# Lane inverse of a gated delta rule: block products associated as (X22 M) X11 instead of X22 (M X11)

## The chip, the cores and the metric

The kernel runs on one core of a Trainium2 chip. The metric is the time of one execution on the device in microseconds (us). The profile names the engines PE (matmul; PEld is its weight load, which overlaps it), DVE (the vector engine), ACT (the scalar engine), POOL (GpSimd) and SP (which issues DMAs). Everything here is in 32-bit floats.

## The reference, cut to what matters

The reference is one transformer block with adaptive layer norm: 8 sequences of 512 rows and 256 columns go through a gated-delta-rule attention and then a mixture of experts with two of six chosen. Only the attention touches the change. For each of its 32 value heads the sequence is cut into chunks, and each chunk needs the inverse of a unit lower triangular matrix:

```
A = -where(strict_tril, einsum('bhnce,bhnde->bhncd', k_beta, kc) * decay, 0)
T = solve_triangular(eye - A, eye, lower=True)
value_      = T @ v_beta
k_cumdecay  = T @ (k_beta * exp(g)[..., None])
```

A scan over the chunks then carries a state of 128 x 128 for each head.

## The kernel before

The kernel uses chunks of 128 rows. A main loop runs over 128 iterations `n`, one for each of 8 sequences and 16 pairs of heads, in a software pipeline. In one turn of the loop it works on the keys of iteration n+9 (`keys`), on one quarter of a lane inverse (`diagonal_blocks`), on joining the inverse of iteration n+1 to full size (`join`), on the values of n+1 (`values`), on the recurrence of n (`recur`), and on the output of n-1 (`finish`). Each of these is a list of steps. `weave` (L52) merges the lists by their relative position, so that the steps of all of them alternate in the queues of the engines; the program's scheduler then settles the order of the single instructions. [...]

**The lane inverse.** One iteration has 2 heads and 4 chunks, so 8 matrices of 128 x 128, each with four 32 x 32 blocks on its diagonal. Four iterations make a group: 4 x 8 x 4 = 128 diagonal blocks. `leave` in `keys` (L648) writes them to DRAM, and `begin` (L707) reads them back so that each of the 128 lanes (partitions) holds one whole 32 x 32 block in `tl`, 1024 floats. DVE then inverts all 128 blocks at once, by elementwise products and sums along the free dimension. There are 32 such groups. `tl` holds a 32 x 32 block of A, called M here, transposed: element [c, r] of `tl` is element [r, c] of M. Two tiles hold the inverse: `xl` holds X by rows, and `yl` holds its transpose, so a row of `yl` is a column of X.

The inverse is built in four quarters, one for each turn of the loop:

- quarter 0: `begin`, then `row(1)` to `row(7)` (L714), which solve the four 8 x 8 blocks on the diagonal into `yl`, and `turn8` (L724), which copies them transposed into `xl`
- quarter 1: `join8_w` and `join8_x`, twice each, which join 8 x 8 blocks to 16 x 16
- quarter 2: `join16_w`, three times, the first product of the join from 16 to 32
- quarter 3: `join16_x`, three times, the second product, and `leave` (L773), which writes `xl` and `yl` to DRAM for `join`

A join fills the lower left block of an inverse whose diagonal blocks X11 and X22 are known: X21 = X22 M X11. Each of the two matrix products is done by a DVE multiplication of broadcast operands into `prl` (`e["pr"]`, up to 1024 products on each lane), and a DVE reduction over the innermost axis. The intermediate is kept in `wt`. Before the change, `join8_w` and `join16_w` form W = M X11, and `join8_x` and `join16_x` form X22 W. The helper `minus_m` (L698) returns a block of M from `tl` with its axes exchanged, so that the innermost axis, the one summed over, steps by one row of `tl`, 32 floats:

```
            def minus_m(r0, c0, nr, ncol):

                return part(e["t"], c0, r0, ncol, nr).rearrange("p c r -> p r c")
```

The lines that later sections name: L721 and L722 (product and reduction of `row`), L727 (`turn8`), L735 and L740 (product and reduction of `join8_w`), L751, L752 and L753 (product, reduction and transposed copy of `join8_x`), L760 and L765 (`join16_w`), L770 and L771 (`join16_x`), L775 (transposed copy in `leave`). Around them on DVE stand the convolutions (L513), the recurrence (`r` L927, `wd` L950, `st` L970 and L973, `o` L988 and L990), the output (`gt` L1046, the sum L1058), and one small instruction for each iteration at L1030.

Of the kernel before, what the change touches and what calls it, by code (L numbers as in the profile page):

```python
# [11 lines left out]
ALU = mybir.AluOpType  # L12
AX = mybir.AxisListType
# [49 lines left out]
def adaln_block(  # L63
# [369 lines left out]
    with ExitStack() as st:  # L433
# [11 lines left out]
        xl = w1b.tile([P, 32, 32], F32, name="xl")  # L445
        yl = w1b.tile([P, 32, 32], F32, name="yl")
# [234 lines left out]
        def diagonal_blocks(g):  # L681


            e = {}
            mul, red = nc.vector.tensor_tensor, nc.vector.tensor_reduce
            flat = lambda t: t.rearrange("p a b -> p (a b)")

            def part(t, r0, c0, nr, ncol):
                return t[:, r0 : r0 + nr, c0 : c0 + ncol]

            def diag8(t, r, c, nr, ncol):

                a = flat(t)
                return bass.AP(
                    a.tensor, a.offset + 32 * r + c, [list(a.ap[0]), [264, 4], [32, nr], [1, ncol]]
                )

            def minus_m(r0, c0, nr, ncol):  # L698

                return part(e["t"], c0, r0, ncol, nr).rearrange("p c r -> p r c")  # L700

            def bc(ap, axis, n):
                shape = list(ap.shape)
                shape.insert(axis, n)
                return ap.unsqueeze(axis).to_broadcast(shape)

            def begin():  # L707
                t = w1b.tile([P, 32, 32], F32, name=f"tl_{g}", tag="tl")
                nc.sync.dma_start(flat(t), groups[g]["t"])
                e["t"] = t  # L710
                e["wt"] = w1b.tile([P, 256], F32, name=f"wt_{g}", tag="wt")
                e["pr"] = w1b.tile([P, 1024], F32, name=f"prl_{g}", tag="prl")

            def row(i):  # L714
                y = diag8(yl, 0, i, i, 1)
                m = diag8(e["t"], 0, i, i, 1)
                if i == 1:
                    nc.vector.tensor_copy(y, m)
                    return
                pr = e["pr"][:, : 4 * i * i].rearrange("p (q c b) -> p q c b", q=4, c=i)  # L720
                mul(pr, diag8(yl, 0, 0, i, i), m.rearrange("p q b o -> p q o b").to_broadcast([P, 4, i, i]), ALU.mult)  # L721
                red(y.rearrange("p q c o -> p q (c o)"), pr, AX.X, ALU.add)  # L722

            def turn8():  # L724
                a = flat(xl)
                src = flat(yl)
                nc.vector.tensor_copy(  # L727
                    bass.AP(a.tensor, a.offset, [list(a.ap[0]), [264, 4], [32, 8], [1, 8]]),
                    bass.AP(src.tensor, src.offset, [list(src.ap[0]), [264, 4], [1, 8], [32, 8]]),
                )  # L730

            def join8_w(q):
                o = 16 * q
                pr = e["pr"][:, 512 * q : 512 * q + 512].rearrange("p (c a b) -> p c a b", c=8, a=8)
                mul(  # L735
                    pr, bc(minus_m(o + 8, o, 8, 8), 1, 8), bc(part(yl, o, o, 8, 8), 2, 8),
                    ALU.mult,
                )
                if q == 1:
                    red(  # L740
                        e["wt"][:, :128], e["pr"][:, :1024].rearrange("p (x b) -> p x b", b=8),
                        AX.X, ALU.add,
                    )

            def join8_x(q):
                o = 16 * q
                wt = e["wt"][:, 64 * q : 64 * q + 64].rearrange("p (c b) -> p c b", c=8)
                pr = e["pr"][:, 512 * q : 512 * q + 512].rearrange(
                    "p (a c b) -> p a c b", a=8, c=8
                )  # L750
                mul(pr, bc(part(xl, o + 8, o + 8, 8, 8), 2, 8), bc(wt, 1, 8), ALU.mult)  # L751
                red(part(xl, o + 8, o, 8, 8), pr, AX.X, ALU.add)  # L752
                nc.vector.tensor_copy(  # L753
                    part(yl, o, o + 8, 8, 8), part(xl, o + 8, o, 8, 8).rearrange("p a c -> p c a")
                )

            def join16_w(c, n, b):

                pr = e["pr"].rearrange("p (c a b) -> p c a b", c=n, a=16)
                mul(  # L760
                    pr, bc(minus_m(16, b, 16, 16 - b), 1, n), bc(part(yl, c, b, n, 16 - b), 2, 16),
                    ALU.mult,
                )
                wt = e["wt"].rearrange("p (c a) -> p c a", c=16)
                red(wt[:, c : c + n, :], pr, AX.X, ALU.add)  # L765

            def join16_x(a, n, w):
                pr = e["pr"].rearrange("p (a c b) -> p a c b", a=n, c=16)
                wt = e["wt"].rearrange("p (c b) -> p c b", c=16)
                mul(pr, bc(part(xl, 16 + a, 16, n, w), 2, 16), bc(wt[:, :, :w], 1, n), ALU.mult)  # L770
                red(part(xl, 16 + a, 0, n, 16), pr, AX.X, ALU.add)  # L771

            def leave():  # L773
                nc.sync.dma_start(groups[g]["x"], flat(xl))
                nc.vector.tensor_copy(  # L775
                    part(yl, 0, 16, 16, 16), part(xl, 16, 0, 16, 16).rearrange("p a c -> p c a")
                )
                nc.sync.dma_start(groups[g]["y"], flat(yl))

            return [  # L780
                [begin, *[lambda i=i: row(i) for i in range(1, 8)], turn8],
                [lambda: join8_w(0), lambda: join8_w(1), lambda: join8_x(0), lambda: join8_x(1)],
                [lambda: join16_w(0, 4, 0), lambda: join16_w(4, 4, 0), lambda: join16_w(8, 8, 8)],
                [
                    lambda: join16_x(0, 8, 8), lambda: join16_x(8, 4, 16),
                    lambda: join16_x(12, 4, 16), leave,
                ],
            ]

# [285 lines left out]
        for n in range(-LA, last + 2):  # L1075
# [18 lines left out]
            g, q = divmod(n + LA, 4)  # L1094
            if 0 <= g - 1 <= last // 4:
                if q == 0:
                    quarters = diagonal_blocks(g - 1)
                streams.append(quarters[q])
# [58 lines left out]
```

## Time and profile before

| | us |
|---|---|
| median of 3 runs | 4919.81 |
| lowest and highest of these | 4910.78, 4920.14 |
| the profiled execution's own time | 4912.86 |
| its span, from the first to the last instruction | 4911.1 |
| DVE busy in the products and reductions of the joins, L735 to L771 | 729.2 |

The last row sums the groups of those lines that have TENSOR_TENSOR or TENSOR_REDUCE as their operation. The granted clock of PE was 0.965 of full speed on average. The page of a profile gives each engine's busy time and how it is spread over the span; groups of instructions by line, with the mean duration of one; and the waits, that is, which instruction of which engine was late for which. Line numbers are those of the kernel before.

### The profile page before, as it was taken

How to read it: one execution, taken by the hardware profiler on the slowest of the kernel's cores; microseconds unless marked ns; L12 is line 12 of the kernel's file. 1: busy time of each engine (PE TensorE's matmuls, PEld its weight loads, DVE VectorE, ACT ScalarE, POOL GpSimd, SP SyncE). 2: the span in 40 equal slices, each digit the busy share in tenths (PEclk: the TensorE clock that was granted, in tenths of full speed). 3: DMA queues.
4: the chain of work that ended last, by engine and by line, in shares of the span. 5: the costliest groups of instructions: out<-in, count | busy, mean ns of one | idle time of the engine just before them, and what ended most of it. 6: DMA issues, size and time to landing. Idle time of an engine off the chain costs nothing. (4 is left out here: it accounts for less than half of the span.)

```text
span 4911.1 us, 84235 instructions
## 1 busy us (share of the span) xinstructions
PE 4569.8 (93%) x27112; PEld 3262.1 (66%) x27112; DVE 3815.8 (78%) x8513; ACT 3120.0 (64%) x8899; POOL 1826.3 (37%) x1708
## 2 busy tenths in 40 slices
PE   5599999999999999999999999999999999999998
PEld 3366666666666666676666666666666666666775
DVE  4678878877878778888788887788877887878864
ACT  4566666666666666676666665666755666666553
POOL 3333434334333334334334343333333334333311
PEclk8689999999999999999999999999999999999998
DMA  5555555555555555555454555555555555556431
GB/s 154 120 142 146 145 160 150 155 145 155 151 144 155 150 151 143 141 157 159 150 158 143 146 163 147 144 157 146 160 138 145 149 151 154 140 148 158 133 107 46
DMA packets 1045671, 712.91 MB, mean 145 GB/s; under 512 B 661105, under 2 KB 909809, under 8 KB 1045233
## 3 DMA queue, kind: packets, MB, share of 16 engines
q1 hardware_dynamic: 1044416, 705.69, 52.7%
q8 instruction: 219, 3.59, 0.3%
q14 instruction: 220, 1.79, 0.1%
q10 hardware_dynamic: 816, 1.84, 0.1%
HBM read 459.27 MB, written 247.99 MB: 144 GB/s over the span
## 5 line engine op out<-in xcount | busy, mean ns | idle before, releaser
L513 DVE SCALAR_TENSOR_TENSOR cvv<-prv,cw,cvv 128x511 f32<-128x511 f32 (+2 forms) x768 | 560.5, 742 | 19.8 <-ACT cvv L511 18.3
L996 ACT ACTIVATE jo<-o 128x128 f32<-128x128 f32 x1024 | 304.5, 298 | 386.1 <-DVE o L990 350.9
L1031 POOL TENSOR_TENSOR msq<-msq,mhalf 128x8 f32<-128x8 f32 x128 | 223.3, 1744 | 876.6 <-DVE msq L1030 758.4
L1053 PE MATMUL op<-wo,gt 128*128 128x256 f32 x2048 | 504.9, 385 | 28.4 <-DVE gt L1046 21.8
L1021 PE MATMUL prz<-ha,wz 128*128 128x512 f32 x1024 | 496.7, 607 | 14.8 <-DMA wz<-in_dram 12.0
L637 POOL TENSOR_TENSOR mta<-mta,dca 128x512 f32<-128x512 f32 x256 | 326.3, 1275 | 466.6 <-DVE mta L626 429.4
L503 PE MATMUL prv<-ha,wv 128*128 128x512 f32 x1024 | 492.9, 603 | 4.9 <-DVE cvk L513 4.7
L604 ACT ACTIVATE dca<-gb,G 128x128 f32<-128x128 f32 x1024 | 334.8, 392 | 239.5 <-DMA sfar<-dca 179.8
L1053 PEld LDWEIGHTS op<-wo,gt 128*128 128x128 f32 x2048 | 370.6, 191 | 101.5 <-DVE gt L1046 37.4
L956 ACT ACTIVATE w<-u,br 128x128 f32<-128x128 f32 x1024 | 320.5, 361 | 164.3 <-DVE wd L950 130.0
L567 POOL TENSOR_TENSOR nrmk<-nrmk,half 128x4 f32<-128x4 f32 x128 | 140.9, 1101 | 741.3 <-ACT jk L563 727.5
L639 POOL TENSOR_TENSOR dca<-qkm,dca 128x256 f32<-128x256 f32 x512 | 387.6, 778 | 18.7 <-DVE qkm L631 0.6
L982 PEld LDWEIGHTS in<-w,s 128*128 128x128 f32 x2048 | 312.4, 197 | 92.7 <-issue 55.5
L982 PE MATMUL in<-w,s 128*128 128x128 f32 x2048 | 337.4, 287 | 4.3 <-ACT w L956 4.3
L617 PE MATMUL kk<-kqa 128*128 128x256 f32 x1024 | 314.2, 419 | 26.0 <-ACT kqa L527 14.6
L964 PE MATMUL dst<-wd,kr 128*128 128x256 f32 x768 | 265.7, 428 | 77.0 <-DVE wd L950 52.2
L513 DVE SCALAR_TENSOR_TENSOR cvk<-prk,cw,cvk 128x511 f32<-128x511 f32 (+2 forms) x384 | 285.8, 744 | 60.8 <-ACT cvk L511 57.8
L555 POOL TENSOR_TENSOR sq<-kqa 128x512 f32<-128x512 f32 x128 | 135.8, 1061 | 530.3 <-ACT kqa L527 530.3
L513 DVE SCALAR_TENSOR_TENSOR cvq<-prq,cw,cvq 128x511 f32<-128x511 f32 (+2 forms) x384 | 285.6, 744 | 40.6 <-ACT cvq L511 39.0
L503 PEld LDWEIGHTS prv<-ha,wv 128*128 128x128 f32 x1024 | 187.4, 192 | 182.8 <-issue 169.7
L941 PEld LDWEIGHTS u<-r,y 128*128 128x128 f32 x1536 | 235.7, 192 | 106.4 <-issue 51.9
L941 PE MATMUL u<-r,y 128*128 128x128 f32 x1536 | 291.2, 293 | 15.9 <-DVE r L927 15.1
(218 smaller groups left out, 11310.3 us busy)
## 6 DMA issues: line engine op xcount, KB each, us to landing
gb<-gfar SPq DMA_DIRECT2D x128, 512.0 KB
qfar<-kqa SPq DMA_DIRECT2D x128, 512.0 KB
kq<-qfar SPq DMA_DIRECT2D x128, 512.0 KB
sfar<-dca SPq DMA_DIRECT2D x256, 256.0 KB
s<-sfar SPq DMA_DIRECT2D x128, 512.0 KB
wk<-in_dram SPq DMA_DIRECT2D x256, 128.0 KB
wv<-in_dram SPq DMA_DIRECT2D x128, 256.0 KB
wz<-in_dram SPq DMA_DIRECT2D x128, 256.0 KB
```

Of the source, the lines that this page charges most:

```text
L503: mm(ps, d[wname][:, kt, j * P : (j + 1) * P], hT[:, kt, :], start=kt == 0, stop=kt == NKT - 1,)
L513: nc.vector.scalar_tensor_tensor(a[:, s:], ps[:, : SEQ - s], cw[:, ch, 3 - s : 4 - s], a[:, s:], ALU.mult, ALU.add,)
L604: nc.scalar.activation(dc[:, c, h, :], d["gb"][:, 2 * gr + c, h * P : (h + 1) * P], AF.Relu, bias=rw["G"][:, 2 * gr + c, k : k + 1], scale ...
L617: mm(ps[:, c2 * 2 * P : (c2 + 1) * 2 * P], d["kqa"][:, c, 0, :], d["kqa"][:, c].rearrange("p k i -> p (k i)"), start=True, stop=True,)
L637: nc.gpsimd.tensor_tensor(mt, mt, dc.rearrange("p c h i -> p (c h) i"), ALU.mult)
L639: nc.gpsimd.tensor_tensor(dc[:, c], bc_mid(d[f"qkm{gr}"][:, c, :], 2), dc[:, c], ALU.mult)
L941: mm(ps[:, h * P : (h + 1) * P], d["y"][:, 2 * c + h, :], r[:, h, :], start=True, stop=True,)
L956: nc.scalar.activation(w[:, h, :], ps[:, h * P : (h + 1) * P], AF.Copy, scale=d["br2"][:, c, h : h + 1],)
L982: mm(ps[:, h * P : (h + 1) * P], d["s"][:, 2 * c + h, :], cur["w"][:, h, :], start=True, stop=True,)
L996: nc.scalar.activation(junk, d["o"][:, c, h, :], AF.Square, accum_out=d["msq"][:, c, h : h + 1])
L1021: mm(ps, d["wz"][:, kt, h * P : (h + 1) * P], hT[:, kt, :], start=kt == 0, stop=kt == NKT - 1,)
L1053: mm(ps[:, k * DM : (k + 1) * DM], gt[h][:, c * P : (c + 1) * P], d["wo"][:, h, :], start=h == 0, stop=h == 1,)
```

## The change

The joins form W = X22 M first and then W X11. The first product multiplies rows of `xl` (rows of X22) with rows of `tl` (columns of M). The second multiplies rows of `wt` with rows of `yl` (columns of X11). `minus_m` is no longer used and is removed. `wt` now holds W by rows [a, b]. Since X22 and X11 are lower triangular, the calls with shortened sums change places: `join16_w` takes rows of X22 in portions of 8, 4 and 4 with sums over 8, 16 and 16 elements, and `join16_x` takes columns of X11 in portions of 4, 4 and 8 with sums over 16, 16 and 8. Every product still has 512 or 1024 elements per lane, and the number of instructions is the same.

```diff
             def join8_w(q):
                 o = 16 * q
-                pr = e["pr"][:, 512 * q : 512 * q + 512].rearrange("p (c a b) -> p c a b", c=8, a=8)
+                pr = e["pr"][:, 512 * q : 512 * q + 512].rearrange("p (a b r) -> p a b r", a=8, b=8)
                 mul(
-                    pr, bc(minus_m(o + 8, o, 8, 8), 1, 8), bc(part(yl, o, o, 8, 8), 2, 8),
+                    pr, bc(part(xl, o + 8, o + 8, 8, 8), 2, 8), bc(part(e["t"], o, o + 8, 8, 8), 1, 8),
                     ALU.mult,
                 )
...
             def join8_x(q):
...
-                mul(pr, bc(part(xl, o + 8, o + 8, 8, 8), 2, 8), bc(wt, 1, 8), ALU.mult)
+                mul(pr, bc(wt, 2, 8), bc(part(yl, o, o, 8, 8), 1, 8), ALU.mult)
                 red(part(xl, o + 8, o, 8, 8), pr, AX.X, ALU.add)
...
-            def join16_w(c, n, b):
-
-                pr = e["pr"].rearrange("p (c a b) -> p c a b", c=n, a=16)
+            def join16_w(a, n, w):
+
+                pr = e["pr"].rearrange("p (a b r) -> p a b r", a=n, b=16)
                 mul(
-                    pr, bc(minus_m(16, b, 16, 16 - b), 1, n), bc(part(yl, c, b, n, 16 - b), 2, 16),
+                    pr, bc(part(xl, 16 + a, 16, n, w), 2, 16), bc(part(e["t"], 0, 16, 16, w), 1, n),
                     ALU.mult,
                 )
-                wt = e["wt"].rearrange("p (c a) -> p c a", c=16)
-                red(wt[:, c : c + n, :], pr, AX.X, ALU.add)
-
-            def join16_x(a, n, w):
-                pr = e["pr"].rearrange("p (a c b) -> p a c b", a=n, c=16)
-                wt = e["wt"].rearrange("p (c b) -> p c b", c=16)
-                mul(pr, bc(part(xl, 16 + a, 16, n, w), 2, 16), bc(wt[:, :, :w], 1, n), ALU.mult)
-                red(part(xl, 16 + a, 0, n, 16), pr, AX.X, ALU.add)
+                wt = e["wt"].rearrange("p (a b) -> p a b", a=16)
+                red(wt[:, a : a + n, :], pr, AX.X, ALU.add)
+
+            def join16_x(c, n, b):
+
+                pr = e["pr"].rearrange("p (a c b) -> p a c b", a=16, c=n)
+                wt = e["wt"].rearrange("p (a b) -> p a b", a=16)
+                mul(
+                    pr, bc(wt[:, :, b:], 2, n), bc(part(yl, c, b, n, 16 - b), 1, 16), ALU.mult
+                )
+                red(part(xl, 16, c, 16, n), pr, AX.X, ALU.add)
...
-                [lambda: join16_w(0, 4, 0), lambda: join16_w(4, 4, 0), lambda: join16_w(8, 8, 8)],
+                [lambda: join16_w(0, 8, 8), lambda: join16_w(8, 4, 16), lambda: join16_w(12, 4, 16)],
                 [
-                    lambda: join16_x(0, 8, 8), lambda: join16_x(8, 4, 16),
-                    lambda: join16_x(12, 4, 16), leave,
+                    lambda: join16_x(0, 4, 0), lambda: join16_x(4, 4, 0),
+                    lambda: join16_x(8, 8, 8), leave,
                 ],
```

More of the change, by code (lines that the diff above doesn't have):

```diff
@@ L696, in diag8 @@
                 )
-            def minus_m(r0, c0, nr, ncol):
-                return part(e["t"], c0, r0, ncol, nr).rearrange("p c r -> p r c")
             def bc(ap, axis, n):
@@ L740, in join8_w @@
                     red(
-                        e["wt"][:, :128], e["pr"][:, :1024].rearrange("p (x b) -> p x b", b=8),
+                        e["wt"][:, :128], e["pr"][:, :1024].rearrange("p (x r) -> p x r", r=8),
                         AX.X, ALU.add,
@@ L746, in join8_x @@
                 o = 16 * q
-                wt = e["wt"][:, 64 * q : 64 * q + 64].rearrange("p (c b) -> p c b", c=8)
+                wt = e["wt"][:, 64 * q : 64 * q + 64].rearrange("p (a b) -> p a b", a=8)
                 pr = e["pr"][:, 512 * q : 512 * q + 512].rearrange(
```

## The prediction

> **What bounds the kernel now.** I read the page's busy shares first, then the groups of instructions by line with shapes kept apart, then windows cut at the lane inverse, then the waits of the tensor engine (PE).
>
> The page's first part:
>
> ```profile
> span 4911.1 us, 84235 instructions
> PE 4569.8 (93%) x27112; PEld 3262.1 (66%) x27112; DVE 3815.8 (78%) x8513; ACT 3120.0 (64%) x8899; POOL 1826.3 (37%) x1708
> ```
>
> PE looks like the bound, but a busy PE counts each matmul to its modelled end, and these overlap. So 93% does not say that PE issues back to back. DVE, at 78%, is the only other engine near full, and 78% is an average over stages.
>
> The lane inverse runs once per group of four iterations, 32 times. Cutting four groups at the start of their first step (L718, at 1983.1, 2128.0, 2276.5 and 2422.3 us in the trace) and halving each shows those stages. The windows give, for PE, PEld, DVE, ACT and POOL, busy us and number of instructions:
>
> ```profile
> 1983.00:2056.00 73.00, 67.77 (x385) 47.92 (x385) 65.00 (x150) 44.77 (x134) 29.79 (x28) 0.95 0.51 137
> 2056.00:2128.00 72.00, 69.96 (x445) 50.97 (x444) 56.07 (x124) 50.28 (x144) 26.60 (x26) 1.00 0.52 159
> 2128.00:2201.00 73.00, 68.63 (x424) 49.45 (x422) 65.93 (x162) 48.43 (x139) 27.36 (x26) 1.00 0.56 135
> 2201.00:2276.00 75.00, 72.77 (x437) 51.36 (x436) 57.71 (x134) 53.31 (x158) 28.03 (x27) 1.00 0.60 177
> 2276.00:2349.00 73.00, 69.87 (x425) 49.00 (x423) 63.92 (x132) 48.18 (x127) 30.36 (x25) 0.98 0.50 143
> 2349.00:2422.00 73.00, 70.20 (x421) 51.62 (x419) 46.31 (x104) 47.74 (x135) 26.60 (x26) 0.95 0.49 151
> 2422.00:2495.00 73.00, 70.19 (x405) 50.23 (x406) 65.72 (x139) 44.42 (x134) 28.17 (x26) 0.98 0.54 144
> 2495.00:2566.00 71.00, 68.31 (x435) 49.22 (x434) 53.46 (x121) 47.90 (x143) 28.14 (x27) 1.00 0.55 154
> ```
>
> The first half of each group, where nearly all of the lane inverse runs, has DVE busy 260.6 of 292 us (89%); the second half 213.6 of 291 us (73%). The first halves retire 1639 matmul records in 292 us (5.61 per us), the second halves 1738 in 291 us (5.97 per us). PE's work per iteration is the same in both, so the stretch with the full DVE moves about 6% slower. It is not stopped: most of what DVE does there is hidden.
>
> The waits of PE say through what a late DVE is felt:
>
> ```profile
> PE dst L964 <- DVE wd L950: 52.2, 35, 3.6
> PE pi L919 <- DVE st L970: 34.2, 39, 2.4
> PE op L1053 <- DVE gt L1046: 21.8, 28, 1.7
> PE u L941 <- DVE r L927: 15.1, 26, 1.5
> ```
>
> These are steps of the recurrence and of the output. DVE works its queue in order, so a product of the inverse ahead of `wd`, `st`, `r` or `gt` holds it, and PE after it.
>
> [...]
>
> **The change part by part.** Groups by line with shapes kept apart (busy us, mean ns of one | idle before):
>
> ```profile
> L760 DVE TENSOR_TENSOR prl<-tl,yl 128x1024 f32<-128x1024 f32 x96 | 186.0, 1938 | 0.0
> L770 DVE TENSOR_TENSOR prl<-xl,wt 128x1024 f32<-128x1024 f32 x96 | 117.2, 1221 | 0.3
> L735 DVE TENSOR_TENSOR prl<-tl,yl 128x512 f32<-128x512 f32 x64 | 65.9, 1045 | 0.0
> L751 DVE TENSOR_TENSOR prl<-xl,wt 128x512 f32<-128x512 f32 x64 | 45.3, 711 | 0.0
> L752 DVE TENSOR_REDUCE xl<-prl 128x64 f32<-128x512 f32 x64 | 43.7, 682 | 0.2
> L771 DVE TENSOR_REDUCE xl<-prl 128x64 f32<-128x1024 f32 x64 | 77.5, 1210 | 0.0
> L771 DVE TENSOR_REDUCE xl<-prl 128x128 f32<-128x1024 f32 x32 | 38.6, 1207 | 0.0
> ```
>
> The reader sees two pairs of equal work. L760 and L770 both multiply 1024 elements from SBUF; only L760 walks one operand down a column of `tl`, 128 bytes per step. It costs 717 ns more. L735 against L751 costs 334 ns more for half the elements. That is 0.70 and 0.65 ns per element: a price per element read, not per instruction.
>
> 1. *The first products (join16_w, 3 per group; join8_w, 2 per group).* Both operands are now read along rows: rows of `xl` repeated over the columns, against rows of `tl` repeated over the rows. That is the pattern of L770 and L751 with `tl` in `wt`'s place, so I take their durations: 96 x (1938 - 1221) = 68.8 us and 64 x (1045 - 711) = 21.4 us less. Bounds: nothing gained, if row steps of 32 elements in the second operand cost what column steps do (`xl` already has such rows in L770 as the first operand, which speaks against it); and no more than the 90.2 us.
> 2. *The second products (join16_x, join8_x).* Rows of `wt` against rows of `yl`; before, rows of `xl` against rows of `wt`. The runs are still 8 or 16 elements. Cost 0, with a bound of a few per cent of 117.2 + 45.3 us, say 5 us either way.
> 3. *The reductions.* As many elements go in. The last ones write `xl` in runs of 4 or 8 instead of 16. L752 writes runs of 8, and 1024 against 512 input elements cost 1210 against 682 ns, 1.03 ns per input element; 64 or 128 results give the same 1210 and 1207 ns. What is written is not seen in the price, so 0, bound 3 us.
> 4. *What is moved.* `join8_w` now needs `xl` and so the copy of `turn8`, which stood ahead of it in the same queue: no new wait. No DMA, buffer, matmul or semaphore partner is added or removed; `tl` and `wt` have the same lifetimes. The queue order differs, since the program's scheduler places instructions by its own estimate: set against each other, the PE queues differ in 4299 lines, mostly neighbours swapped. On DVE the stretch from the first step of a group to its last copy holds 182 instructions on average after, 187 before. I cost this at 0 and keep it for the rivals.
>
> Sum on DVE: 3815.8 - 90.2 = 3725.6 us, all of it in the crowded halves: 2.82 us per group out of about 65.
>
> What of that reaches the end? The crowded halves have (260.6 - 213.6) / 4 = 11.7 us more DVE work and run 6% slower, 4.4 us of 73. In proportion, 2.82 us less work is worth 4.4 x 2.82 / 11.7 = 1.06 us per group, 34 us for 32 groups. The price at the margin may be higher, since the last work added to a nearly full queue costs most; or lower, since the next late thing is ACT (`w` L956 before `in`, `kqa` L527 before `kt`, 37.2 us of PE's waits) and PE's own issue. I take 34 us. The profiled execution took 4912.9 us (span 4911.1), so 4879 us by its own measure; the median of the runs shown is 6.9 us higher, which would give 4886. I put the forecast between, at **4882 us**.
>
> **Rivals.**
>
> *Full gain.* In the crowded half DVE is the bound, and all 90 us come off: 4916 - 90 = 4826, with 4916 the middle of the two times before. For it: DVE at 89%, no idle time ahead of L760 and L735 (0.0), so nothing absorbs the shortening at once. Against it: PE is still at 5.61 of 5.97 matmuls per us there, so at most 4.4 us per group, 141 us, is there to win, and much of that lies in waits for ACT.
>
> *Hidden.* DVE idles 11% of even the crowded half, and the time saved only lengthens its waits: `wd` waits 75.7 us for `u`, `o` 78.1 us for `in`. Then the time stays within 10 us of 4916. Against it: in the timeline DVE runs from 2040.1 to 2051.4 us without a gap, with one L760 in that stretch, and PE does wait for DVE.
>
> *Slower, by the new order.* The place is the recurrence, where PE `dst` waits for `wd`: 52.2 us over 35 waits, 1.5 us each. If the rearranged queues put a product or reduction of the inverse (1.2 us) ahead of `wd` or `st` where there was none, each such place costs about 1.5 us of PE. From 34 / 1.5 = 23 more of them over 128 iterations the gain is gone; with 60 it is 4916 - 34 + 90 = 4972 us. For it: the order differs from the first groups on. Against it: the inverse keeps its length in the queue, its place in the iterations, and each of its instructions is shorter or equal.
>
> *The column read is not the cause.* If L760 is slow for another reason (for instance that `tl` is one operand, in a bad place beside `yl`), the first products stay at 1938 ns and the time at 4916. L735 showing the same price per element at another shape and offset speaks against it; it shares the chance of the hidden case.
>
> **How the numbers follow.** Partial gain, the forecast: 0.62, its own range 4855 to 4902. Full gain or near it: 0.17. Hidden, or the price not as read: 0.12. Slower by order: 0.09. A measurement of this kernel can tell about 0.2%, 10 us, from no change. Partial and full together give faster 0.79, and 0.01 of the hidden case falls there too: 0.80; same 0.11; slower 0.09. The range takes the partial case with most of the full gain and of the hidden case, 4840 to 4916.
>
> **What would show it.** In the profile after: the first products at about 1220 and 700 ns (step 1); the second products and reductions unchanged within 2% (2 and 3); DVE busy near 3726 us; matmuls per us in the crowded halves up by some 1.5%; the waits of `dst`, `pi` and `op` for DVE shorter in sum. A first product that stays above 1.5 us makes step 1 wrong. DVE 90 us less busy at an unchanged span makes the share wrong; DVE 90 us less busy and a longer span with longer waits of `dst` or `pi` for DVE is the order's doing.

## The result, and the profile after

| | before | after |
|---|---|---|
| median of 6 runs, us | 4919.98 | 4888.33 |
| lowest to highest, us | 4910.78 to 4933.35 | 4880.04 to 4893.0 |
| the profiled execution, us | 4912.86 | 4891.77 |

The ratio is 0.9933, with a 95% interval of 0.9915 to 0.9952: 32 us less. The forecast, 4882 us, is 38 us below the median of before; the prediction's own sum was 34 us.

The first lines of the page of the kernel after:

```profile
span 4890.1 us, 84160 instructions
PE 4564.2 (93%) x27112; PEld 3254.2 (67%) x27112; DVE 3765.9 (77%) x8513; ACT 3116.2 (64%) x8899; POOL 1811.7 (37%) x1708
```

DVE is busy for 49.9 us less, not for the 90.2 us of the sum. The groups of the joins by line, shapes kept apart, say whether the products are to blame (busy us, mean ns of one | idle before). In the kernel after, L732 and L737 are join8_w, L748 to L750 join8_x, L757 and L762 join16_w, L768 and L771 join16_x:

```profile
L757 DVE TENSOR_TENSOR prl<-xl,tl 128x1024 f32<-128x1024 f32 x96 | 119.1, 1240 | 0.0
L768 DVE TENSOR_TENSOR prl<-wt,yl 128x1024 f32<-128x1024 f32 x96 | 118.3, 1233 | 0.1
L577 DVE TENSOR_SCALAR nrm<-nrm 128x4 f32<-128x4 f32 x128 | 85.8, 670 | 118.5 <-POOL nrm L576 116.9
L771 DVE TENSOR_REDUCE xl<-prl 128x64 f32<-128x1024 f32 x64 | 77.2, 1207 | 0.2
L748 DVE TENSOR_TENSOR prl<-wt,yl 128x512 f32<-128x512 f32 x64 | 49.4, 774 | 0.0
L732 DVE TENSOR_TENSOR prl<-xl,tl 128x512 f32<-128x512 f32 x64 | 43.0, 687 | 0.1
```

They are not. The first products fell from 186.0 + 65.9 to 119.1 + 43.0 us, 89.8 us less. Part of what came back is elsewhere: L577, a line that the change does not touch, rose from 66.2 us (517 ns each) to 85.8, and the product that is now L748 from 45.3 to 49.4. Other lines became shorter, so that the durations of all DVE records fell by 78 us in sum, from 4383.6 to 4305.4. The other 28 us are a matter of counting: the records of neighbouring instructions overlap, the page counts an overlap once, and the overlap fell from 567.8 to 539.4 us.

PE's waits for DVE at the four places shown of before, and one that has grown (us in total, times, longest):

```profile
PE dst L964 <- DVE wd L950: 53.5, 43, 3.7
PE op L1053 <- DVE gt L1046: 30.0, 27, 2.1
PE op L1053 <- DVE o L990: 28.6, 30, 2.0
PE pi L919 <- DVE st L970: 15.4, 23, 2.4
PE u L941 <- DVE r L927: 10.4, 14, 1.6
```

The wait for the state `st` is down from 34.2 to 15.4 us, while `op` waits more: for `gt` 30.0 (21.8 before) and for `o` 28.6 (5.9). In sum, PE's waits for DVE hardly fell: 228.0 us before, 225.3 after. So two things happened at once, shorter products and another order of the queues. The experiments take them apart.

The windows, cut as before at the starts of four groups and at their middles, first halves shown:

```profile
1975.00:2047.00 72.00, 67.86 (x403) 47.60 (x402) 63.37 (x150) 45.54 (x136) 28.62 (x27) 0.98 0.53 142
...
2118.00:2193.00 75.00, 69.65 (x403) 49.68 (x401) 65.61 (x161) 45.22 (x130) 28.19 (x25) 0.95 0.48 128
...
2268.00:2338.00 70.00, 66.72 (x401) 47.44 (x400) 62.05 (x131) 48.26 (x132) 26.59 (x26) 0.98 0.48 138
...
2409.00:2483.00 74.00, 71.30 (x446) 51.56 (x443) 65.17 (x144) 46.70 (x139) 29.02 (x27) 1.00 0.56 152
```

DVE is still busy for 256.2 of 291 us (88%) there, and 1653 matmuls in 291 us make 5.68 per us, against 5.61. Single halves range from 5.37 to 6.03 per us, so a difference as small as this one is not clear of their spread.

### The profile page after: what moved, and what is told of

It reads as the page before. It is cut to its first block, busy times and chain, and to the rows that moved or that the text cites. A ratio compares the mean times of both kernels' runs of the same rounds, so it can differ in the third digit from the quotient of the medians.

```text
span 4890.1 us, 84160 instructions
## 1 busy us (share of the span) xinstructions
PE 4564.2 (93%) x27112; PEld 3254.2 (67%) x27112; DVE 3765.9 (77%) x8513; ACT 3116.2 (64%) x8899; POOL 1811.7 (37%) x1708
## 3 DMA queue, kind: packets, MB, share of 16 engines
q1 hardware_dynamic: 1044416, 705.69, 53.5%
## 5 line engine op out<-in xcount | busy, mean ns | idle before, releaser
L513 DVE SCALAR_TENSOR_TENSOR cvv<-prv,cw,cvv 128x509 f32<-128x509 f32 (+2 forms) x768 | 563.1, 741 | 20.2 <-ACT cvv L511 19.2
L1053 PE MATMUL op<-wo,gt 128*128 128x256 f32 x2048 | 516.0, 391 | 63.2 <-DVE gt L1046 30.0
L1031 POOL TENSOR_TENSOR msq<-msq,mhalf 128x8 f32<-128x8 f32 x128 | 233.1, 1821 | 860.2 <-DVE msq L1030 750.2
L567 POOL TENSOR_TENSOR nrmk<-nrmk,half 128x4 f32<-128x4 f32 x128 | 129.7, 1014 | 673.5 <-ACT jk L563 652.3
L964 PE MATMUL dst<-wd,kr 128*128 128x256 f32 x768 | 266.2, 429 | 61.9 <-DVE wd L950 53.5
L941 PEld LDWEIGHTS u<-r,y 128*128 128x128 f32 x1536 | 241.3, 194 | 94.8 <-issue 41.4
```

Source lines behind the costliest of these rows:

```text
L513: nc.vector.scalar_tensor_tensor(a[:, s:], ps[:, : SEQ - s], cw[:, ch, 3 - s : 4 - s], a[:, s:], ALU.mult, ALU.add,)
L941: mm(ps[:, h * P : (h + 1) * P], d["y"][:, 2 * c + h, :], r[:, h, :], start=True, stop=True,)
L1053: mm(ps[:, k * DM : (k + 1) * DM], gt[h][:, c * P : (c + 1) * P], d["wo"][:, h, :], start=h == 0, stop=h == 1,)
```

## The experiments

The theory at the start was that of the prediction: the column read is dear, and its price reaches the end because it stands in the crowded half of a group. The first rival was that the new order of the queues made the gain. Ratios are to the kernel before, run on the same chip, with 95% intervals. The median of before was 4921.65 us beside e1 to e4, 4927.09 beside e5 to e8 and 4932.16 beside e9 to e12, so ratios are compared, not times; the expectations count from 4920 us. Each kernel that exchanges the axes of a block (M or X22 enters transposed) computes another matrix than the reference asks for, with the same amount of work. It has the order of the kernel that it is made from, in the queues of PE and DVE, so that only the reading differs.

**e1: rows in the old order.** One line of the kernel before:

```diff
-                return part(e["t"], c0, r0, ncol, nr).rearrange("p c r -> p r c")
+                return part(e["t"], c0, r0, nr, ncol)
```

> The kernel before, with one edit: the first products read the block of tl by rows, without exchanging its axes (so M enters transposed; the products are otherwise as before). The order of instructions in every queue is that of before. Theory (the price of the column read): L760 falls to about 1230 ns, L735 to about 700 ns, and the time falls by the whole of what the change gave, about 32 us, to 4888. Rival (the new order of the queues made the gain): the products get shorter and the time stays at 4920.

Measured: 4887.85 us, ratio 0.9928 (0.9906 to 0.9951). The same groups of e1:

```profile
L760 DVE TENSOR_TENSOR prl<-tl,yl 128x1024 f32<-128x1024 f32 x96 | 117.1, 1219 | 0.0
L735 DVE TENSOR_TENSOR prl<-tl,yl 128x512 f32<-128x512 f32 x64 | 43.1, 688 | 0.0
```

and PE's waits for DVE in e1:

```profile
PE dst L964 <- DVE wd L950: 53.5, 36, 3.3
PE pi L919 <- DVE st L970: 22.2, 25, 2.2
PE op L1053 <- DVE gt L1046: 20.2, 24, 1.7
PE u L941 <- DVE r L927: 12.6, 19, 1.6
```

Without a change of order, the shorter products give as much as the whole change does. In the same queue the wait of `pi` for `st` falls from 34.2 to 22.2 us, that of `u` for `r` from 15.1 to 12.6; `dst` and `op` hardly move. PE's waits for DVE fall to 203.2 us in all, 25 less than before; about half of that is the state of the recurrence, which stands in DVE's queue behind products of the inverse. A late instruction on DVE holds those behind it, as one place in the trace of before shows: DVE stood idle for 1.96 us ahead of L575, which waited for PE, until 2063.04 us, and L771 behind it started at 2063.12 us, though the product it sums, the L770 that started at 2055.67 us, had taken only 1.22 us. The kernel after is as fast with 225.3 us of such waits, so the lists of waits do not show by which path the gain reaches the end there. The rival falls, as far as the gain of the change itself goes.

**e2 and e5: columns in the new order.** The changed kernel with the block of `tl` (e2) or of `xl` (e5) read down its columns; in `join16_w` (and likewise in `join8_w`):

```diff
-                    pr, bc(part(xl, 16 + a, 16, n, w), 2, 16), bc(part(e["t"], 0, 16, 16, w), 1, n),
+                    pr, bc(part(xl, 16 + a, 16, n, w), 2, 16), bc(part(e["t"], 0, 16, w, 16).rearrange("p r b -> p b r"), 1, n),
```

> The changed kernel, with one edit: the first products read the block of tl by columns (so M enters transposed). The order of instructions in every queue is that of the changed kernel. Theory: the first products are back at about 1940 and 1040 ns and the time is back at 4920, within 10 us. Rival (order): the time stays at about 4888. If the new order costs something that the shorter products paid for, the time is above 4920.

> The changed kernel in its own order of the queues; the first operand of the first products, the block of xl, is read by columns (X22 enters transposed), as in the kernel before the first operand was. If column reads are dearer in the new order than in the old one, as e2 suggests, the time is again near 4944. If e2's extra came from having the column read in the second operand, the time is near that of before, 4920.

Measured: e2 4944.5 us, ratio 1.0042 (1.0025 to 1.0060); e5 4954.35 us, ratio 1.0051 (1.0031 to 1.0071). Both are slower than before. The large first products take 1971 and 1972 ns, hardly more than the 1938 of before, so it does not matter which operand goes down the column. With columns, then, the new order is 0.4 to 0.5% worse than the old one; with rows it is as good (0.9933 against 0.9928). What a column read costs the kernel depends on the order of the queues.

**e3 and e4: a second helping, elsewhere.** In the old order the second products read their block of `xl` by columns too, with the first products by columns (e3) or by rows (e4):

```diff
-                mul(pr, bc(part(xl, 16 + a, 16, n, w), 2, 16), bc(wt[:, :, :w], 1, n), ALU.mult)
+                mul(pr, bc(part(xl, 16, 16 + a, w, n).rearrange("p b a -> p a b"), 2, 16), bc(wt[:, :, :w], 1, n), ALU.mult)
```

> The kernel before, with the second products too reading their block of xl by columns (so X22 enters transposed), in the order of before: some 90 us more of DVE work on top of before. If DVE time is worth the same share as in the change, 0.35, the time rises by 32 us to about 4952. If the share grows with the load on DVE, it rises by 45 to 90 us, to 4965 or more. Rival (DVE time is hidden): it stays within 10 us of 4920.

> The first products by rows and the second products by columns (M and X22 enter transposed), in the order of before: the DVE work of before, but its slow reads moved to the second products, of which more than half run in the emptier part of a group. If only the amount of DVE work counts, the time is that of before, 4920. If the place counts, it is below, about 4900.

Measured: e3 4943.49 us, ratio 1.0047 (1.0033 to 1.0060); e4 4906.12 us, ratio 0.9966 (0.9950 to 0.9983). In e3 the second products take 187.5 + 68.9 us in place of 117.2 + 45.3, 94 us more, for 0.47% or 23 us: a share of 0.25, where the first products had 0.39 (35 us by e1, of 92). It does not grow with the load on DVE here, though the intervals of the two prices, 7 us about the 23 and 11 us about the 35, overlap. e4 lies between e1 and before, as the sum of e1 and e3 would have it. That the later place is cheaper fits the theory, but the intervals allow equal shares too.

**e6 and e7: the inverse spread over the group.** The changed kernel with edges of order in the program. `pin` forbids the scheduler to issue an instruction ahead of the one traced before it on the same engine; no wait is added.

```diff
+            pin = tc.keep_in_program_order
...
-                mul(
+                i = mul(
                     pr, bc(part(xl, 16 + a, 16, n, w), 2, 16), bc(part(e["t"], 0, 16, 16, w), 1, n),
                     ALU.mult,
                 )
+                if a == 0:
+                    pin(i)
```

e6 pins the first product of each of quarters 1 to 3, e7 (without the `if`) every product of the joins.

> The changed kernel with an edge of order alone (no wait): the first product of each of quarters 1 to 3 may not be issued ahead of the DVE instruction traced before it. This moves join8_w from the last half iteration of quarter 0's turn to the next turn, join16_w and join16_x by about one half to a whole turn later, so that the inverse is spread over the whole group in place of its first half. Theory (crowding: a DVE instruction costs time because it stands in a nearly full stretch of the queue): 15 to 60 us faster than the changed kernel, 4830 to 4875. Rival (only the amount of DVE work counts): 4888. Second rival (the inverse is late for the join that follows at once): slower than 4920.

> As e6, with every product of the joins held behind the DVE instruction traced before it. Theory (crowding): as e6 or a little better, 4830 to 4875. Second rival (the inverse is late): above e6, with PE waiting for the data of the join.

Measured: e6 4948.62 us, ratio 1.0045 (1.0034 to 1.0057); e7 4921.45 us, ratio 0.9992 (0.9981 to 1.0003). The theory fails here. e6 is as slow as the second rival said, but a late inverse does not show: PE's waits for DMA are 9.6 us in e6, 7.0 in the kernel after and 15.8 before. What grew in e6 is the wait of `op` for `gt`, 97.9 us against 30.0. The windows of e7, halves of the first two groups from 1985 us on (PE, PEld, DVE, ACT, POOL):

```profile
1985.00:2059.00 74.00, 68.68 (x422) 49.49 (x422) 59.21 (x143) 44.77 (x123) 28.27 (x27) 0.95 0.54 140
2059.00:2133.00 74.00, 70.33 (x420) 49.65 (x420) 58.94 (x130) 50.09 (x148) 27.84 (x26) 1.00 0.58 148
2133.00:2208.00 75.00, 69.61 (x443) 49.67 (x441) 59.94 (x159) 50.52 (x137) 27.04 (x26) 1.00 0.53 143
2208.00:2283.00 75.00, 71.11 (x404) 49.45 (x405) 60.64 (x128) 48.92 (x152) 29.86 (x27) 0.98 0.61 172
```

The spreading worked: DVE is at 80% in these four halves and at 74 to 78% in the next four, where in the kernel before it went from 89 to 73%. There is no crowded half left, and the kernel is 0.6% slower than the changed one. PE's waits for DVE add up to 251.0 us in e7, against 225.3 in the kernel after. The largest, of `vt` for `qkm` (below), is new: the kernel after has none of that pair. The first products are longer too, though they read rows: 1488 ns for the large ones, against 1240. No run shows why.

**e8: columns in the pinned order**, the edit of e2 on e7.

> As e7, in the same order of the queues, with the block of tl read by columns in the first products (M enters transposed): some 90 us more of DVE work than e7. Theory (crowding): the column read costs less here than the 34 us of the old order, at most 20 us over e7. Rival (only the amount counts): 34 us or more over e7.

Measured: 4996.99 us, ratio 1.0155 (1.0128 to 1.0182), 1.63% or 80 us over e7. The dearest place for the column read so far is one where DVE is evenly loaded. The large first products take 2215 ns, 727 more than in e7, so the read itself costs what it does elsewhere. Waits of PE in e7, then in e8 (the lines of this kernel stand 7 later):

```profile
PE vt L897 <- DVE qkm L631: 50.8, 31, 2.6
PE op L1060 <- DVE gt L1053: 50.7, 44, 2.7
PE dst L971 <- DVE wd L957: 38.4, 37, 3.1
PE u L948 <- DVE r L934: 18.8, 38, 1.6
```

```profile
PE op L1060 <- DVE gt L1053: 54.6, 47, 2.8
PE dst L971 <- DVE wd L957: 50.9, 40, 3.1
PE u L948 <- DVE r L934: 38.6, 63, 1.4
PE pi L926 <- DVE st L977: 13.7, 24, 1.9
```

`r` and `wd` are waited for 20 and 12 us more, and `st` (L977), which is not in e7's list, now costs 13.7: the recurrence again. In the order of the DVE records, 214 instructions of the steps `residual` and `update` stand directly behind an instruction of a join in e7; in the kernels before and after it is 38 and 40. That led to the next theory: what counts is how often a join stands directly ahead of the recurrence.

**e10, e11, e12: other orders of the same work.** e10 gives three steps of the recurrence a higher priority in the scheduler; e11 gives the join steps a lower one, in the same way with the offset -300; e12 is e11 with the edit of e2.

```diff
+            def first(step, c):
+                with tc.high_priority(offset=200):
+                    step(c)
...
-                    steps.append(lambda c=c: residual(c))
+                    steps.append(lambda c=c: first(residual, c))
...
-                steps.append(lambda c=c: weigh(c))
+                steps.append(lambda c=c: first(weigh, c))
...
-                    steps.append(lambda c=c: update(c))
+                    steps.append(lambda c=c: first(update, c))
```

> The changed kernel with the steps residual, weigh and update of the recurrence given a higher priority in the program's scheduler; same instructions. In the order of DVE's queue 130 of 768 steps of residual and update then stand directly behind an instruction of a join, where it was 33 (and 214 in e7). Theory (what counts is how often a join stands directly ahead of the recurrence): slower than the changed kernel, between it and e7, 4895 to 4925. Rival (a recurrence that is issued as soon as it is ready loses less): faster than 4888.

> The changed kernel with the join steps given a lower priority in the program's scheduler; same instructions, and they stay in the same halves of the group (42 steps of residual and update directly behind a join). Theory (order matters only through such places): within 15 us of 4888. Rival (the new order of the change is an unlucky one of several): 10 to 30 us faster.

> As e11, in the same order, with the block of tl read by columns in the first products (M enters transposed): 90 us more of DVE work. The price of the column read in this order: 34 us over e11 if it is as in the old order, 57 us as in the new one, 80 us as in the pinned one. Theory (few joins directly ahead of the recurrence): 30 to 60 us.

Measured: e10 4864.78 us, ratio 0.9868 (0.9843 to 0.9892); e11 4900.36 us, ratio 0.9939 (0.9917 to 0.9961); e12 4988.46 us, ratio 1.0113 (1.0088 to 1.0138).

e10 is faster than the changed kernel with 131 such neighbours, so counting them does not explain the times; the rival named beside it holds. The waits of `pi` for `st` (L970 and L973) are down to 7.4 us. PE's waits in e10:

```profile
PE dst L964 <- DVE wd L950: 41.4, 44, 3.8
...
PE prv L503 <- DVE cvk L513: 36.7, 31, 2.9
PE u L941 <- DVE r L927: 26.2, 20, 2.1
...
PE op L1057 <- DVE gt L1050: 12.3, 14, 1.9
```

Compared with the kernel after, `wd` and `gt` are waited for less (41.4 for 53.5, 12.3 for 30.0), the convolution `cvk` more (36.7 for 3.6): other work has become late instead. The sum for DVE is nearly the same, 223.4 us against 225.3, so these waits do not show where e10's gain comes from. e11 is no better than the change, as expected. e12 costs 1.74% or 86 us over e11, beyond the 30 to 60 us of the second theory. PE's clock moved with it: on average it was granted 0.956 in the runs of e12 and 0.965 in those of e11, which by the relation given in the last section goes with some 31 us. In e8 it hardly moved, 0.970 against 0.972 in e7, and the price was 80 us all the same.

**e9: less work.** The changed kernel with shorter sums in one portion of each 16 join, and the 8 x 8 step solved by columns of X from the last to the first, so that it reads along rows:

```diff
-                y = diag8(yl, 0, i, i, 1)
-                m = diag8(e["t"], 0, i, i, 1)
+                k = 7 - i
+                x = diag8(xl, k + 1, k, i, 1)
+                m = diag8(e["t"], k, k + 1, 1, i)
...
-                mul(pr, diag8(yl, 0, 0, i, i), m.rearrange("p q b o -> p q o b").to_broadcast([P, 4, i, i]), ALU.mult)
+                mul(pr, diag8(xl, k + 1, k + 1, i, i), m.to_broadcast([P, 4, i, i]), ALU.mult)
...
-                [lambda: join16_w(0, 8, 8), lambda: join16_w(8, 4, 16), lambda: join16_w(12, 4, 16)],
+                [lambda: join16_w(0, 8, 8), lambda: join16_w(8, 4, 12), lambda: join16_w(12, 4, 16)],
...
-                    lambda: join16_x(0, 4, 0), lambda: join16_x(4, 4, 0),
+                    lambda: join16_x(0, 4, 0), lambda: join16_x(4, 4, 4),
```

> The changed kernel with less DVE work in the same inverse: the third portion of each 16 join sums over 12 elements in place of 16 (768 products in place of 1024, in join16_w and in join16_x), and the 8 x 8 step solves X by columns from the last to the first, so that it reads rows of tl and xl. Estimate from the prices of before: 2 x 2 x 256 x 1.04 ns x 32 = 34 us less in products and reductions, and 556 elements x 0.65 ns x 32 = 12 us less in the 8 x 8 step, 46 us in all. At a share of 0.37 the time is 17 us below the changed kernel, 4871; if the share in its new order is 0.6, 4860; if the order it comes in is a bad one, 4890 or above.

Measured: 4867.18 us, ratio 0.9865 (0.9839 to 0.9890). With the prices of before, 1.00 ns for an element of a product and 1.03 for one of a reduction, the first term of the estimate is 33 us. DVE is busy for 3722.0 us, 43.9 less than in the kernel after; the ratio fell by 0.68%, 33 us, with an interval of 16 us either way. Of the shares expected, 0.6 of 46 us (28 us) lies within it and 0.37 (17 us) at its edge. e9 and e10 both beat both kernels, by different means; the two together were not tried.

The price of the same column read, about 90 us of DVE time, in each order (differences of the ratios times 4920 us; from the intervals of the ratios, a price is known to 11 to 16 us):

| order of the queues | rows | columns | price, us | share |
|---|---|---|---|---|
| before | 0.9928 (e1) | 1 | 35 | 0.4 |
| changed | 0.9933 (after) | 1.0042, 1.0051 (e2, e5) | 54, 58 | 0.6 |
| joins last | 0.9939 (e11) | 1.0113 (e12) | 86 | 0.95 |
| joins pinned | 0.9992 (e7) | 1.0155 (e8) | 80 | 0.9 |

One path was left out of the experiments. With the column read POOL is busy longer too, by the pages of all four pairs, for the same 1708 instructions: 1826.3 us before and 1791.6 in e1, 1839.8 in e2 and 1811.7 after, 1848.6 in e8 and 1811.7 in e7, 1856.9 in e12 and 1805.8 in e11. In e12 most of it is the scaling of `o` ahead of the output, 314.8 us against 281.7. PE itself waits for POOL less than 4 us in each of them, and times on POOL are rough; whether part of the price goes through POOL is open.

## Why the prediction was right, and where it was not

*Step 1, the first products.* Right: 89.8 us less, forecast 90.2. Each of them ended within 25 ns of the durations taken. e1 to e5 show the cause too: reading a column is what costs, on either operand (for 1024 elements 1219 ns by rows in e1, 1971 and 1972 by columns in e2 and e5), and so the rival that the column read is not the cause falls. Why a column costs more, no run here shows. For the price along rows, the two row products of before give an estimate: (1221 - 711) / 512 = 1.00 ns per element and a fixed part of about 200 ns.

*Steps 2 and 3.* The reductions stayed (L771 1207 ns). The large second products took 1233 for 1221 ns; the small ones 774 for 711, 9% more and outside the 2% named, but 4.1 us in sum, within the bound of 5.

*Step 4, the moved order, costed at 0.* For the time of the change that holds: e1 and the kernel after are 0.5 us apart, with intervals of about 10 us. As a reading of the order it was too simple. The order gave DVE 28 us more to do (3765.9 against 3737.8 in e1, 19.6 of it in L577), which is most of the miss against the forecast of 3726 us; and it makes column reads dearer (54 and 58 us against 35). The changed kernel does not pay for that, since its first and second products read no column any more.

*The share.* The size, 0.38 of the DVE time saved (34 of 90 us), was right: 35 us by e1. The reason given for it was not. It took the slower progress of the crowded half as what DVE work costs in proportion. e7 removes the crowded half and gains nothing; e8 then makes the same work cost 80 us. The share changes with the order of the queues and does not follow the load of a stretch, and that the proportion gave 0.38 was luck. The reading that nearly all of the inverse runs in the first half was too wide as well: all first products do, but in the windows shown 8.2 of the 14.6 us of the large second products (L770) fall in second halves. That matmuls per us would rise by some 1.5% in the crowded halves came out near, at 1.2%, but within the spread of single halves.

*The waits, named as a sign.* Those of `dst`, `pi` and `op` for DVE were to be shorter in sum. They were not: over all lines of DVE they come to 142.8 us before and 141.9 after. `dst` and `pi` fell, and `op` rose by as much. In e1, in the old order, they come to 124.0. So the path named, through the recurrence, fits e1, and for the change itself it is not shown.

*The rivals.* The full gain did not come, though nearly the full price was measured in e8 and e12, in other orders. Hidden: refuted by e1. Slower by order: not for this change, yet e6 shows that an order can cost 1.1%, more than the change gains.

## What to carry to other kernels

Look for vector products that walk an operand down a column in the free dimension, and price them against a product of the same shape that reads rows, in the same profile; here that difference, 90.2 us in sum, was right to 1% (89.8). Do not take a stage's busy share as the price of its work: the same 90 us cost 35 to 86 us, depending on the order of the queues. Where a scheduler places the instructions, test an edit in the old order too, and try the order itself: giving the recurrence priority took off as much again as the edit had (0.65% and 0.67%).

## What the runs showed that was not expected

The time follows the granted clock of PE from run to run. In 41 runs of the kernel before, from 4896 to 4949 us, the correlation with the mean clock (0.957 to 0.970) is -0.94, with 36 us for each 0.01; in 44 runs on another chip it is -0.85, with 35 us. Between kernels the clock does not order the times: e7 has the highest, 0.972, and is no faster than before (ratio 0.9992). The clock records in the traces of before and after hold nothing but 1.0 and 0.5, in stretches that alternate. Whether stalls of PE and a lower clock go together is not shown: from e11 to e12 PE's waits for DVE grew by 37 us and the mean clock fell from 0.965 to 0.956, from e7 to e8 they grew by 57 us and it fell only from 0.972 to 0.970.

A TENSOR_SCALAR on 4 elements (L577) took 517 ns on average before, 670 after and 669 in e2, which shares the order of the kernel after; in e1, in the old order, it took 517 again. Its minimum is 158 ns before. It follows on a POOL instruction on the same tile (L576), for which DVE stood idle 105.3 us in all before and 116.9 after. So the order made it slow; by which mechanism, no run here shows.

What stays open is why the old order forgives the column read most. In each of the four pairs PE's waits for DVE rise with the column read, by 25 us (e1 to before), 29 (after to e2), 37 (e11 to e12) and 57 (e7 to e8). That is less than the price each time and not in its order, and a count of neighbours in the queue does not explain the prices either.
